# One conditioned transformer block on one core: half of the MLP's transposed rows are modulated by ScalarE instead of VectorE

## The chip, the core and the metric

The kernel runs on one core of one Trainium2 chip. The core has five engines that work beside each other: TensorE (PE, matrix products and transposes; PEld is its load of stationary operands), VectorE (DVE), ScalarE (ACT), GpSimd (POOL) and SyncE (SP), which issues most of the transfers. Each engine takes its own instructions in the order in which the program gives them, and semaphores hold an instruction back until those that it depends on, on other engines, have ended. Matrix products are written into PSUM, here in banks of 128 x 512 float32, and another engine carries them from there to SBUF.

The metric is the device time of the whole program in microseconds (us). It is the median of several executions; one more execution is taken with the hardware profiler.

## The reference: what is computed

The input x has 4 sequences of 1024 rows of 512 numbers, and each sequence has one conditioning vector of 512. First comes a graph attention layer over 20 neighbours per row. Its result goes through a transformer block that is modulated by the condition:

```python
mod = jax.nn.silu(c) @ W_mod + b_mod
sh_msa, sc_msa, g_msa, sh_mlp, sc_mlp, g_mlp = jnp.split(mod, 6, axis=-1)
x = x + g_msa * _attention(_modulate(_layernorm(x), sh_msa, sc_msa), W_qkv, W_out, b_out)
x = x + g_mlp * _ff(_modulate(_layernorm(x), sh_mlp, sc_mlp), W1, b1, W2, b2)
```

`_modulate(x, shift, scale)` is `x * (1 + scale) + shift`, with one shift and one scale for each of the 512 features of a sequence. `_ff` is `gelu(x @ W1 + b1) @ W2 + b2` with 2048 hidden features. The change concerns the modulation in the last of these lines. All is in float32.

## The kernel before

The kernel runs through three stages on the one core: the graph layer, the attention (with 16 heads, planned step by step by a list of fillers), and the MLP. The change lies in the MLP, which fills the last 780 us of the profile.

**Blocks.** The MLP goes over the 4096 rows in `NB2` = 8 blocks of 512 rows (`VB` = 4 tiles of 128 rows), in the loop over `k` at L1486. Each block has two parts on PE. The *up* part multiplies the block's rows with W1, in four groups `p`; the first two groups of block 0 were already done in the attention stage, so block 0 has only groups 2 and 3 here. The *down* part multiplies the hidden values with W2.

**Seven products.** Each group of the up part, and the whole down part, is a two by two block product that is done with seven products instead of eight (`seven`, L484). Its steps are a, c, b, a2, b2, d, b3, in that order on PE (`with_four`, L528). The up part uses the four PSUM banks `mau`, `mbu`, `mcu`, `mdu`, and the down part has four of its own, `mad`, `mbd`, `mcd`, `mdd`. In the up part a step has 8 products of 128 x 256, and in the down part it has 32. Step a ends with a copy of bank a to bank b by ScalarE (L519), and step c with a copy to SBUF, also by ScalarE (L508). The other banks are carried out by VectorE (L511, L515, L1539, L1544). The sums of operands that the seven products need are made by VectorE (`up_sums` L633, with L468 to L471) and by GpSimd (`mlp_rows` L600, with L476). In block 0 VectorE also makes the sums of W2 once (eight instructions at L476 that write `w2x` and `w`).

**The next block's rows.** While block k runs, the rows of block k+1 are loaded into `xl` (L379) and normalized in place by VectorE (`norm_rows`, L389). They then have to stand with features on the partitions, in the tile `hT`. That is done in `between()` (L1520), which is called right after step a of the down part has been emitted (L1552 to L1555). For each of the `FC` = 4 chunks of 128 features `norm_T` (L397) puts four transposes on PE (L407), which fill one PSUM bank, and one instruction that reads the bank, multiplies by the scale, adds the shift and writes the chunk of `hT`:

```python
if on_act:
    nc.scalar.activation(hT[st, k][:, c, :], pt, AF.Identity, scale=scale, bias=shift)   # L412
else:
    nc.vector.tensor_scalar(hT[st, k][:, c, :], pt, scale, shift, ALU.mult, ALU.add)     # L414
```

The banks are two of the up part's, which are free at that time. `new_bank` (L1475) gives them in turn: chunks 0 and 2 are transposed into `mcu`, chunks 1 and 3 into `mau`. So the transposes of chunk 2 wait until chunk 0 has been read, and those of chunk 3 until chunk 1 has been read. Since PE takes its instructions in order, step c of the down part (bank `mcd`) stands behind all sixteen transposes.

After the transposes `between()` gives SP the loads of the block's residual rows (`rows2`, L1530; these reuse the buffers of `xl`, so they wait for the transposes that read them), GpSimd the four sums of `mlp_rows` over the new `hT`, and then GpSimd four additions of a bias to the residual rows (L1534). The sums are needed by the up part of the next block, the residual rows by L1544 at the end of steps a2, b2, d and b3.

**Order.** The order of the instructions on each engine is that of the program's text: the schedule is written by hand. Block 7 has no next rows, so there are 7 places where `norm_T` is called in the MLP, for k = 0 to 6. `norm_T` is also used for the attention's rows and for the MLP's first rows; there it is called with its default, `on_act=True`.

Of the kernel before, what the change touches and what calls it, by code (L numbers as in the profile page):

```python
# [41 lines left out]
def cond_block_kernel(  # L42
# [71 lines left out]
    def rstd(rs, mv, nm, a, b):  # L114

        nc.scalar.activation(rs[:, a:b], mv[:, a:b, 1], AF.Sqrt, bias=eps)
        nc.vector.reciprocal(rs[:, a:b], rs[:, a:b])
        nc.vector.scalar_tensor_tensor(nm[:, a:b], mv[:, a:b, 0], -1.0, rs[:, a:b], ALU.mult, ALU.mult)

    def spread(k, b, o):  # L120

        nc.sync.dma_start(o, gated[32 * k + b : 32 * k + b + 1, :].broadcast_to([P, F]))
# [9 lines left out]
    with ExitStack() as gctx:  # L132
# [243 lines left out]
        def norm_load(st, k):  # L376
            for i in range(k * VB, (k + 1) * VB):
                t = rp.tile([P, F], F32, name="xl", tag="xl", bufs=VB)
                nc.sync.dma_start(t, NORM[st][0][i])  # L379
                xl[st, i] = t  # L380
# [12 lines left out]
        def norm_rows(st, k, on_act=False):  # L393
            for i in range(k * VB, (k + 1) * VB):
                norm_row(st, i, on_act)

        def norm_T(st, k, c, bank, on_act=True):  # L397

            sh, sc = NORM[st][4:]
            b = k * VB // NT  # L400
            if st == 1 and k > 0:
                hT[st, k] = hT[st, 0]
            elif c == 0:
                hT[st, k] = rp.tile([P, FC, VB * P], F32, name="hT", tag="hT", bufs=2)
            pt = bank("ptn")
            for n in range(VB):
                nc.tensor.transpose(  # L407
                    pt[:, n * P : (n + 1) * P], xl[st, k * VB + n][:, c * P : (c + 1) * P], ident
                )
            scale, shift = modT[:, sc + c, b : b + 1], modT[:, sh + c, b : b + 1]  # L410
# [4 lines that stand above are left out]
# [58 lines left out]
        def steps_b(e, o, b11, b12, b21, b22):  # L473

            return [
                lambda o=o_, i=i, j=j: e.tensor_tensor(o, i, j, ALU.subtract)  # L476
                for o_, i, j in ((o[0], b12, b11), (o[1], b22, o[0]), (b12, b22, b12), (o[2], b21, o[1]))
            ]
# [49 lines left out]
        def with_four(**kw):  # L528

            parts = seven(**kw)  # L530

            def step(n):
                for f in parts[n]:
                    f()

            return [lambda n=n: step(n) for n in ("a", "c", "b", "a2", "b2", "d", "b3")]
# [63 lines left out]
        def mlp_rows():  # L600

            h = hT[1, 0]
            if "mlp" not in tx:
                tx["mlp"] = xp.tile([P, 6, F], F32, name="tx", tag="tx")
            o = [tx["mlp"][:, k, :].rearrange("p (c r) -> p c r", c=2) for k in range(3)]
            sums_b(nc.gpsimd, o, h[:, :2, :HB], h[:, :2, HB:], h[:, 2:, :HB], h[:, 2:, HB:])
# [5 lines left out]
        def up_lhs(p):  # L612
            return lambda which, q, c: of_weights(2 * p + q, w1g[2 * p + q], which, c)
# [7 lines left out]
        def hidden(p, i, j):  # L621

            k = 2 * (2 * j + i)
            return hs[p][:, k : k + 2, :].rearrange("p q r -> p (q r)")

        def gelu(p, i, j, t):
            o = hidden(p, i, j)
            for q in (1, 0):
                m = i * MC // 2 + 2 * p + q
                cols = slice(q * HB, (q + 1) * HB)  # L630
                nc.scalar.activation(o[:, cols], t[:, cols], AF.Gelu, bias=vecs[:, V_1 + m : V_1 + m + 1])

        def up_sums(p):  # L633
            h = [hs[p][:, 2 * k : 2 * k + 2, :] for k in range(4)]
            sums_a(nc.vector, [hx[p][:, k] for k in range(3)], *h)
# [280 lines left out]
    with ExitStack() as actx:  # L916
# [14 lines left out]
        def bank(name):  # L931
            return ps.tile([P, F], F32, name=name, **MM)
# [40 lines left out]
        def short():  # L973
            return op_.tile([P, F], F32, name="s", tag="s", bufs=1)
# [457 lines left out]
    with ExitStack() as mctx:  # L1432
# [53 lines left out]
        for k in range(NB2):  # L1486
            b = k * VB // NT
            nxt = k + 1
            if nxt < NB2:
                norm_load(1, nxt)  # L1490
            for p in range(2 if k == 0 else 0, 4):
                steps = with_four(
                    get=up_banks.get, short=short, lhs=up_lhs(p), rhs=up_rhs, nk=2,
                    room=lambda: hidden(p, 1, 1), done=lambda i, j, t: gelu(p, i, j, t),
                )
                for n, f in enumerate(steps):
                    f()
                    if k == 0 and n == (4 if p == 2 else 2):

                        for j in ((0, 1) if p == 2 else (2,)):  # L1500
                            up_sums(j)
                if k > 0:
                    up_sums(p)
                elif p == 3:
                    sums = []
                    for j in range(2):
                        o = [w2x[j][:, n] for n in range(3)]
                        q, r = w2s[j], w2s[2 + j]
                        sums.append(steps_b(nc.vector, o, q[:, :, :HB], q[:, :, HB:], r[:, :, :HB], r[:, :, HB:]))
                    for n, two in enumerate(zip(*sums)):  # L1510
                        for f in two:
                            f()
                        if n == 0:
                            up_sums(p)
                if p == 1 and k == 1:
                    rstd(rs2, mv2, nm2, 3 * NT, NTA)
                if p == 2 and nxt < NB2:
                    norm_rows(1, nxt)

            def between():  # L1520
                if nxt < NB2:
                    for c in range(FC):
                        norm_T(1, nxt, c, new_bank, on_act=False)
                if k * VB % NT == 0:
                    spread(2, b, gate2)
                    spread(3, b, bias2)
                for n in range(VB):
                    i = k * VB + n
                    rows2[n] = rp.tile([P, F], F32, name="x2", tag="xl", bufs=VB)
                    nc.sync.dma_start(rows2[n], x2d[i])  # L1530
                if nxt < NB2:
                    mlp_rows()
                for n in range(VB):
                    nc.gpsimd.tensor_tensor(rows2[n], rows2[n], bias2, ALU.add)  # L1534

            def dn_done(i, j, t):
                y = t if (i, j) == (1, 1) else short()
                g = gate2[:, j * HB : (j + 1) * HB].unsqueeze(1).to_broadcast([P, 2, HB])
                nc.vector.tensor_tensor(  # L1539
                    y.rearrange("p (t f) -> p t f", t=2), t.rearrange("p (t f) -> p t f", t=2), g, ALU.mult  # L1540
                )
                for n in range(2):
                    o = rows2[2 * i + n][:, j * HB : (j + 1) * HB]
                    nc.vector.tensor_tensor(o, o, y[:, n * HB : (n + 1) * HB], ALU.add)  # L1544
                    if (i, j) in ((0, 1), (1, 0)):
                        at = k * VB + 2 * i + n
                        nc.sync.dma_start(out[at * P : (at + 1) * P, :], rows2[2 * i + n])

            steps = with_four(
                get=dn_banks.get, short=short, lhs=dn_lhs, rhs=dn_rhs, nk=MC // 2, room=None, done=dn_done  # L1550
            )
            for n, f in enumerate(steps):  # L1552
                f()
                if n == 0:
                    between()  # L1555
# [50 lines left out]
```

## Time and profile before

| | |
|---|---|
| median of 3 runs | 3081.66 us (3077.66 to 3081.82) |
| profiled execution | 3081.5 us, its span 3079.7 us |
| PE busy | 3039.7 us, 99% of the span |
| DVE busy | 1984.5 us, 64% |
| ACT busy | 1421.3 us, 46% |
| POOL busy | 1188.8 us, 39% |
| mean granted TensorE clock | 0.998 |
| L414, DVE, 128 x 512 out of PSUM | 28 instructions, 801 to 811 ns each |
| L412, ACT, the same work in the earlier stages | 36 instructions, 760 to 788 ns each |

The page gives the busy time of each engine, a strip of 40 slices, the chain of work that ended last, and the costliest groups of instructions. The span is the time from the first to the last instruction; the rest of the execution's time lies around it. In the timeline each row holds one instruction or several alike that follow on each other: start, length, engine, line, operation, what it writes and reads, how many, and in square brackets the idle time of that engine before it, with what ended that time. The length of a row of matmuls goes to the modelled end of the last one; the next row can start earlier, since they are pipelined. The granted clock is given as a fraction of the full speed.

### The profile page before, as it was taken

The numbers are of one execution on the slowest core, as the hardware profiler recorded it, in microseconds if no ns is written. First come the engines' busy times: TensorE is split into PE (matmuls) and PEld (weight loads), VectorE is DVE, ScalarE is ACT, GpSimd is POOL, SyncE is SP. The second block draws the span as 40 slices with busy tenths as digits, with TensorE's granted clock in tenths as the row PEclk, the third lists the DMA queues.
The fourth block names the chain that finished last, engine by engine and source line by source line (L and its number), as shares of the span: only waits on it lengthen the run. The fifth ranks groups of instructions, "written<-read, shape, count | busy, mean of one in ns | idle before, by whom it ended". The sixth has DMA issues, their size and how long they took to land.

```text
span 3079.7 us, 40763 instructions
## 1 busy us (share of the span) xinstructions
PE 3039.7 (99%) x14977; PEld 1918.1 (62%) x14977; DVE 1984.5 (64%) x2772; ACT 1421.3 (46%) x2351; POOL 1188.8 (39%) x729
## 2 busy tenths in 40 slices
PE   9999999999999999999999999999999999999999
PEld 5666655455455455455455455455468888888888
DVE  3788867777878777878777877777864332223222
ACT  2344446555655555755555755555641221112211
POOL 1444446445454555454654454654531100111010
PEclk9999999999999999999999999999999999999999
DMA  6343438676877776877776877776872011101110
GB/s 193 117 138 106 134 83 200 158 173 156 198 182 177 181 176 158 198 180 176 183 175 157 199 181 175 187 173 150 194 190 88 21 39 37 48 14 42 35 41 14
DMA packets 281882, 418.00 MB, mean 136 GB/s; under 512 B 28272, under 2 KB 100012, under 8 KB 281684
## 3 DMA queue, kind: packets, MB, share of 16 engines
q1 hardware_dynamic: 281436, 415.05, 53.1%
q8 instruction: 120, 1.97, 0.2%
q14 instruction: 78, 0.64, 0.1%
q10 hardware_dynamic: 248, 0.34, 0.0%
HBM read 121.09 MB, written 25.76 MB: 48 GB/s over the span
## 4 chain that ended last, share of the span: by engine, by line
PE 80%; DVE 7%; ACT 4%; issue 3%; POOL 2%; DMA 2%; SPq 2%; POOLq 0%; ACTq 0%; DVEq 0%
PE q L497 17%; PE psc L1079 14%; PE pav L1041 13%; PE pout L1059 6%; PE mbd L497 5%; PE mbu L497 5%; PE mad L497 3%; PE mau L497 3%; ACT w L1096 2%; PE mcd L497 2%; PE mdd L497 2%; PE mdu L497 2%; PE mcu L497 2%; POOL t L733 1%; DVE mx L1090 1%
## 5 line engine op out<-in xcount | busy, mean ns | idle before, releaser
L1105 POOL TENSOR_SCALAR w<-w,sm 128x1024 f32<-128x1024 f32 x256 | 733.9, 2867 | 874.7 <-DVE sm L1101 874.5
L1096 ACT ACTIVATE w<-psc,mx 128x1024 f32<-128x1024 f32 x512 | 570.6, 1114 | 643.0 <-DVE mx L1090 642.5
L1114 DVE STREAM_TRANSPOSE wd<-w 128x1024 f32<-128x1024 f32 x512 | 633.5, 1238 | 126.1 <-ACT w L1103 111.0
L1090 DVE TENSOR_REDUCE mx<-psc 128x1 f32<-128x1024 f32 x512 | 599.6, 1211 | 119.7 <-PE psc L1079 117.6
L1079 PE MATMUL psc<-kT,qT 64*128 64x512 f32 x2048 | 535.8, 617 | 7.8 <-ACT w L1096 5.0
L1041 PE MATMUL pav<-wT,v 128*64 128x256 f32 x4096 | 475.7, 382 | 1.5 <-DMA wT<-wd 1.4
L1041 PEld LDWEIGHTS pav<-wT,v 128*64 128x64 f32 x4096 | 289.0, 137 | 226.2 <-issue 64.8
L1079 PEld LDWEIGHTS psc<-kT,qT 64*128 64x128 f32 x2048 | 203.5, 186 | 264.3 <-issue 145.3
L1103 ACT ACTIVATE w<-w,sm 128x1024 f32<-128x1024 f32 x256 | 291.0, 1137 | 0.0
L1059 PE MATMUL pout<-wout,oT 128*128 128x512 f32 x512 | 245.6, 609 | 0.0
L476 POOL TENSOR_TENSOR tx<-hT 128x512 f32<-128x512 f32 x8 | 10.2, 1271 | 601.1 <-DVE hT L414 601.1
L497 PE MATMUL q<-hT,wqk 128*128 128x512 f32 (+1 forms) x396 | 182.6, 585 | 4.4 <-DVE q L511 4.4
L1059 PEld LDWEIGHTS pout<-wout,oT 128*128 128x128 f32 x512 | 90.2, 189 | 134.0 <-issue 119.2
L710 PE MATMUL pa<-kp,sfT 128*128 128x320 f32 x512 | 143.5, 433 | 1.4 <-ACT sfT L685 1.4
L519 ACT COPY mbu<-mau 128x512 f32<-128x512 f32 x30 | 17.1, 570 | 276.4 <-PE mau L497 276.4
L1067 DVE TENSOR_TENSOR xr<-pout,xr 128x512 f32<-128x512 f32 x128 | 85.5, 678 | 79.6 <-PE pout L1059 79.5
L497 PEld LDWEIGHTS q<-hT,wqk 128*128 128x128 f32 x396 | 73.5, 190 | 100.7 <-issue 87.3
L497 PE MATMUL q<-tx,ex 128*128 128x512 f32 (+1 forms) x264 | 125.0, 597 | 1.0 <-POOL tx L476 1.0
L710 PEld LDWEIGHTS pa<-kp,sfT 128*128 128x128 f32 x512 | 94.8, 190 | 38.2 <-ACT sfT L685 1.9
L670 PE MATMUL pf<-wx,xT 128*128 128x512 f32 x256 | 116.5, 598 | 0.9 <-DVE pf L659 0.9
L497 PE MATMUL mad<-w,hs 128*128 128x256 f32 x512 | 113.1, 379 | 0.0
L497 PEld LDWEIGHTS mad<-w,hs 128*128 128x128 f32 x512 | 97.3, 190 | 13.2
(285 smaller groups left out, 4221.9 us busy)
## 6 DMA issues: line engine op xcount, KB each, us to landing
wT<-wd SPq DMA_DIRECT2D x1024, 256.0 KB
wqk<-in_w_qkv SPq DMA_DIRECT2D x64, 256.0 KB
xT<-in_xt SPq DMA_DIRECT2D x32, 256.0 KB
xs<-in_x SPq DMA_DIRECT2D x32, 256.0 KB
x1d<-xs SPq DMA_DIRECT2D x32, 256.0 KB
xl<-x1d SPq DMA_DIRECT2D x32, 256.0 KB
wv<-in_w_qkv SPq DMA_DIRECT2D x32, 256.0 KB
xr<-x1d SPq DMA_DIRECT2D x32, 256.0 KB
```

The lines of the kernel that those rows point to most:

```text
L497: nc.tensor.matmul(t[:, q * width : (q + 1) * width], lhsT=lhs(which, q, k), rhs=rhs(which, q, k), start=(fresh and q == 0 and k == 0), st ...
L670: nc.tensor.matmul(pfs[i], lhsT=xT[i][:, c, :], rhs=wx[:, c, :], start=False, stop=(c == FC - 1), skip_group_check=True,)
L710: nc.tensor.matmul(pas[i][:, n, :HF], lhsT=sfT2[i][:, c, :], rhs=kp[:, b, c, n * HF : (n + 1) * HF], start=False, stop=(c == FC - 1), skip ...
L1041: nc.tensor.matmul(po[j * D : (j + 1) * D, :], lhsT=vt[b, g][:, m, p * P + j * D : p * P + (j + 1) * D], rhs=w[:, j, :, m, :], start=(m == 0),
L1059: nc.tensor.matmul(po, lhsT=oT[b, 2 * g + p][:, n * P : (n + 1) * P], rhs=wout[b, g][:, p, :], start=(p == 0), stop=(p == 1),)
L1067: nc.vector.tensor_tensor(t, po, t, ALU.add)
L1079: nc.tensor.matmul(sc[j][:, n * F : (n + 1) * F], lhsT=qT[b, gp][q, t * P : (t + 1) * P], rhs=kT[b, gp][q, n * F : (n + 1) * F], start=Tru ...
L1090: nc.vector.tensor_reduce(mx, sc, axis=AX.X, op=ALU.max, negate=True)
L1096: nc.scalar.activation(w, sc, AF.Exp, bias=mx, accum_out=sm)
L1103: nc.scalar.mul(w, w, sm)
L1105: nc.gpsimd.tensor_scalar(w, w, sm, None, ALU.mult)
L1114: nc.vector.transpose(wd[j][:, :, at, :], wn.pop((b, gp, t, j)).rearrange("p (m k) -> p m k", k=U))
```

## The change

One argument in `between()` changes. Before, all four chunks of the next rows are read out of PSUM by VectorE (L414). After it, block 0 has all four read by ScalarE (L412), and in blocks 1 to 6 chunks 1 and 3 are read by ScalarE and chunks 0 and 2 by VectorE. On ScalarE the new instructions stand between the copy of `mad` to `mbd` (L519) and the copy of `mcd` (L508). The banks, the transposes, PE's order, SP's order and GpSimd's order stay as they were. In number, 16 instructions go from VectorE to ScalarE.

```diff
@@ -1520,7 +1520,7 @@
             def between():
                 if nxt < NB2:
                     for c in range(FC):
-                        norm_T(1, nxt, c, new_bank, on_act=False)
+                        norm_T(1, nxt, c, new_bank, on_act=(k == 0 or c % 2 == 1))
                 if k * VB % NT == 0:
                     spread(2, b, gate2)
                     spread(3, b, bias2)
```

## The prediction

> **What bounds the kernel now.** I read the page first, then the chain of waits, PE's waits, and the timeline around the places that the change touches.
>
> ```profile
> span 3079.7 us, 40763 instructions
> ...
> PE 3039.7 (99%) x14977; PEld 1918.1 (62%) x14977; DVE 1984.5 (64%) x2772; ACT 1421.3 (46%) x2351; POOL 1188.8 (39%) x729
> ...
> PE 80%; DVE 7%; ACT 4%; issue 3%; POOL 2%; DMA 2%; SPq 2%; POOLq 0%; ACTq 0%; DVEq 0%
> ```
>
> PE is busy 99% of the span, and in the MLP the chain that ends last runs along PE from block to block. So the change is worth only what it takes from PE's waits. PE's own waits name the place:
>
> ```profile
> PE mcu L407 <- DVE hT L414: 5.0, 7, 2.2
> ```
>
> Seven times PE waits with a transpose into `mcu` until VectorE has read that bank: 5.0 us in all, 2.2 at the worst. The timeline shows why. First block 0:
>
> ```profile
> 2333.80 0.60 PE L407 MATMUL mcu<-ident,xl 128*128 128x128 f32 x4
> 2333.86 2.35 DVE L476 TENSOR_TENSOR w2x<-w,w2x 128x1024 f32<-128x1024 f32 x2
> 2333.99 0.57 ACT L519 COPY mbd<-mad 128x512 f32<-128x512 f32 x1 [6.07 <-PE mad L497]
> ...
> 2334.23 0.60 PE L407 MATMUL mau<-ident,xl 128*128 128x128 f32 x4
> 2336.13 0.81 DVE L414 TENSOR_SCALAR hT<-mcu,modT 128x512 f32<-128x512 f32 x1
> 2336.85 0.80 DVE L414 TENSOR_SCALAR hT<-mau,modT 128x512 f32<-128x512 f32 x1
> ...
> 2336.99 0.66 PE L407 MATMUL mcu<-ident,xl 128*128 128x128 f32 x4 [2.16 <-DVE hT L414]
> ...
> 2337.71 1.12 PE L407 MATMUL mau<-ident,xl 128*128 128x128 f32 x4
> ...
> 2338.62 8.25 PE L497 MATMUL mcd<-w2x,hx 128*128 128x256 f32 x32
> ...
> 2346.71 7.07 PE L497 MATMUL mbd<-w2x,hx 128*128 128x256 f32 x32
> ```
>
> Call the four groups of transposes T0 to T3 and their reads E0 to E3. T0 is done at 2334.40, but VectorE is busy with the sums of W2 until 2336.21, so T2 starts only at 2336.99. After that wait PE is slow: step c takes 8.09 us to the start of step b instead of 6.91. The granted clock, in windows of that time:
>
> ```profile
> 2337.50:2338.00 0.50, 0.44 (x4) 0.29 (x3) 0.46 (x2) 0.00 (x0) 0.26 (x1) 0.58 0.00 0
> ...
> 2340.00:2341.00 1.00, 1.00 (x4) 0.82 (x3) 0.00 (x0) 0.00 (x0) 1.00 (x1) 0.50 1.02 381
> ```
>
> The third number from the right is the clock: half speed from about 2337.6 to 2341. Windows of 4 us over the whole span show it below 0.995 at three places only, at 88, from 428 and here (0.70 and 0.88 in the two windows from 2336, which is 0.30 x 4 + 0.12 x 4 = 1.68 us lost), and these are the three places after the start where PE idled 2.0 us or more (2.20, 2.00, 2.16); after the next longest idles (1.35, 1.09) it stayed full. Then block 1, which blocks 2 to 6 repeat to within 0.02 us:
>
> ```profile
> 2436.49 0.60 PE L407 MATMUL mcu<-ident,xl 128*128 128x128 f32 x4
> 2436.69 0.57 ACT L519 COPY mbd<-mad 128x512 f32<-128x512 f32 x1 [6.07 <-PE mad L497]
> ...
> 2436.93 0.60 PE L407 MATMUL mau<-ident,xl 128*128 128x128 f32 x4
> 2437.13 0.81 DVE L414 TENSOR_SCALAR hT<-mcu,modT 128x512 f32<-128x512 f32 x1 [5.58 <-PE mcu L407]
> 2437.86 0.80 DVE L414 TENSOR_SCALAR hT<-mau,modT 128x512 f32<-128x512 f32 x1
> ...
> 2438.00 0.66 PE L407 MATMUL mcu<-ident,xl 128*128 128x128 f32 x4 [0.47 <-DVE hT L414]
> ...
> 2438.72 0.65 PE L407 MATMUL mau<-ident,xl 128*128 128x128 f32 x4
> ...
> 2439.21 7.07 PE L497 MATMUL mcd<-w2x,hx 128*128 128x256 f32 x32
> ```
>
> Here VectorE starts E0 0.04 us after T0's end, and E1 right behind E0. T2 starts 0.06 us after E0's end, T3 0.06 after E1's, and step c 0.49 after T3. Groups that follow on each other without a wait stand 0.44 apart (T0 to T1).
>
> **Blocks 1 to 6.** E0 stays on VectorE, so T2 stays at 2438.00. E1 goes to ScalarE, where the copy L519 ends at 2437.26, before T1 does (2436.93 + 0.60 = 2437.53). So E1 starts at about 2437.57. The same instruction in the earlier stages took 760 to 788 ns; with 0.77 E1 ends at 2438.34 and lets T3 go at 2438.40. T3 can't start before T2 has passed, 0.49 after its start: 2438.49. That is now what is late, not the read. Behind T2 without a wait, T3 takes 0.44, so step c starts at 2438.93, against 2439.21: 0.28 us saved in each block, 6 x 0.28 = 1.7 us. E2 and E3 lie beside step c. No row shows both engines reading two banks at once, so bounds: if E1 took 1.09 it would end when VectorE ended it (2438.66) and save 0; below T2's end nothing more is to be had, so 0.28 is the top. I take the top, since all 36 rows of this instruction lie under 0.79, and up to 0.86 would still give it.
>
> [...]
>
> **Block 0.** All four reads go to ScalarE, past the sums of W2. L519 runs from 2333.99 to 2334.56. A second ScalarE instruction starts about 0.10 before the first one's recorded end (266.43 + 0.57 copy, the next at 266.90), so E0 starts at 2334.46, just after T0's end at 2334.40. E0 ends at 2335.23, T2 starts at 2335.29. E1 follows 0.68 behind E0 (1.46 for a row of two), ends at 2335.91, and T3 starts at 2335.97. Step c starts 0.49 later, at 2336.46, against 2338.62: 2.16 saved. PE's wait before T2 becomes 2335.29 - 2334.83 = 0.46 us, like the other blocks' 0.47, after which the clock stayed full six times out of six. So step c takes 6.91 instead of 8.09: another 1.18. Together 3.34 us. The distance between blocks agrees: from T0 of block 0 to T0 of block 1 it is 102.69, between the later ones 99.41.
>
> The bounds are the handover from ScalarE to PE (0.05 to 0.15 us: at 428.26 a ScalarE read ends, its 0.19 us accumulator read at 428.36, and PE goes at 428.41), at most 0.2 us in this block, and the clock: if the slow stretch came all the same, its 1.68 us would be left and the block would save 1.66.
>
> **Waits added or moved.** Step c's first product in block 0 now has a wait on VectorE of its own. Its operands were written by 2329.4; even if it waited for the last sum of W2 (2336.21), that is before 2336.46. Next in line would be this one: it has 0.2 us of cover. L412 waits for PE, and in blocks 1 to 6 for GpSimd's old reads of `hT`, done 90 us before (GpSimd idles 90.37 there). Behind the reads on ScalarE stands only L508, which waits for PE until 2446.32 with 9.05 idle before it; on VectorE L511, idle 13.07. No transfer moves past another: SP's four loads L1530 wait for the transposes, so they go up to 2 us earlier; they and GpSimd's L1534, over by 2449.0, are first read at 2460.93 in block 1. GpSimd's sums start earlier and are needed at 2480. So all of that costs nothing.
>
> **Sum.** 3.34 + 1.68 = 5.0 us. The profiled execution took 3081.5 us (span 3079.7), 0.16 under the median, so the forecast is **3076.5 us**, 0.16% less than before. What a measurement of this kernel can tell from no change is about 0.2%, 6.2 us, so this is just inside.
>
> **Rivals.**
>
> *The clock drops in block 0 anyway.* Then 5.02 - 1.68 = 3.3 us: 3078.2. For it: three cases are few, and the length of the idle time need not be all. Against it: the three longest idle times and the three drops are the same places. [...]
>
> *More is saved than summed.* If PE had no wait at all between T0 and step c, it would take 4 x 0.44 = 1.76 instead of 2.72: 0.96 x 6 + (4.82 - 1.76 + 1.18) = 10.0, or 3071.5. Against it: E0 still has to end before T2. Reads in parallel that hand over earlier would give some of it, 7 us at most: 3074.5.
>
> *The runs fall on the lower level.* One of the three runs shown is 4.0 us under the others, about as much as the drops at 88 and 428 cost together. If the median falls there: 3081.5 - 4 - 5 = 3072.5.
>
> *Slower: ScalarE has to change its function table* between Gelu and this function. A table load is 1283 ns. In blocks 1 to 6 it would run from 2437.26, E1 would end at 2439.31, T3 start at 2439.37, step c at 2439.86: 0.65 lost in each, 3.9 in all, with block 0 still 0.78 better: 3084 to 3085. It gets beyond 0.2% from the point where PE's longer waits also halve the clock in each block (1.68 x 7 more): 3096. Against it: the changed program's ScalarE order holds no further load, and among the 36 earlier ones, that lie between Exp instructions, the profile has none at L412.
>
> **How the numbers follow.** The forecast gets 0.54, the clock drop 0.10, more saved 0.14, the lower level 0.16, the table 0.06. The first two lie within 0.2%, the third and fourth are faster, and the table is slower beyond 0.2% in most of its chance: faster 0.30, same 0.65, slower 0.05. The range runs from the lower level to a little above the clock's case: 3072.0 to 3079.5. The forecast's own range is 3075.7 to 3077.5.
>
> **What would show it.** In the profile after: in block 0 T2 about 1.5 us behind T0, step c 2.66 us behind T0 and 6.91 long, with the clock at 1.00; the distance to the next block's T0 at 99.35 instead of 102.69. In blocks 1 to 6 step c 2.44 us behind T0 instead of 2.72, T3 with no idle time before it, and the distance at 99.13. PE's waits before T2 go from 5.0 us to about 2.8 on L414 (six times) and 0.5 on L412 (once). It would be wrong if E1 on ScalarE took over 1.1 us, if a table load stood at L412 or before the next Gelu, or if the clock fell in another place.

## The result, and the profile after

The changed kernel took 3075.82 us (median of 21 runs, 3071.61 to 3078.84), the kernel before 3079.84 in the same comparison (21 runs, 3073.88 to 3082.91). The ratio is 0.9986, with a 95% interval of 0.9981 to 0.9992: between 2.5 and 5.9 us faster. That is within the 0.2% that the prediction called hard to tell from no change, and the interval of the ratio does not reach 1. The forecast was 3076.5 us and 5.0 us saved. The profiled execution after took 3076.57 us, 4.9 less than the profiled one before.

Two lines of the page after, its span and its busy times:

```profile
span 3074.8 us, 40782 instructions
...
PE 3037.0 (99%) x14977; PEld 1920.7 (62%) x14977; DVE 1971.7 (64%) x2756; ACT 1435.7 (47%) x2367; POOL 1187.5 (39%) x729
```

VectorE lost 16 instructions and 12.8 us of work, ScalarE gained 16 and 14.4 us. Neither number is the gain; PE's waits are. In the list of PE's waits after the change (time in all, times, longest), the group of seven waits with 5.0 us has become these two:

```profile
PE mcu L407 <- DVE hT L414: 2.8, 6, 0.5
...
PE mcu L407 <- ACT hT L412: 0.5, 1, 0.5
```

The timeline of block 0 after the change (start, length, engine, line, operation, what it writes and reads, count, and the idle time before it):

```profile
2333.72 0.60 PE L407 MATMUL mcu<-ident,xl 128*128 128x128 f32 x4
2333.85 2.35 DVE L476 TENSOR_TENSOR w2x<-w,w2x 128x1024 f32<-128x1024 f32 x2
2333.92 0.57 ACT L519 COPY mbd<-mad 128x512 f32<-128x512 f32 x1 [6.06 <-PE mad L497]
...
2334.41 0.79 ACT L412 ACTIVATE hT<-mcu,modT 128x512 f32<-128x512 f32 x1
2335.08 0.79 ACT L412 ACTIVATE hT<-mau,modT 128x512 f32<-128x512 f32 x1
...
2335.25 0.65 PE L407 MATMUL mcu<-ident,xl 128*128 128x128 f32 x4 [0.49 <-ACT hT L412]
...
2335.92 0.66 PE L407 MATMUL mau<-ident,xl 128*128 128x128 f32 x4
...
2336.41 7.07 PE L497 MATMUL mcd<-w2x,hx 128*128 128x256 f32 x32
...
2343.32 2.97 PE L497 MATMUL mbd<-w2x,hx 128*128 128x256 f32 x13
```

VectorE is still busy with the sums of W2, and the reads no longer stand behind them. T2 follows T0 by 1.53 us instead of 3.19, step c follows T0 by 2.69 instead of 4.82, and step c is 6.91 long (2336.41 to 2343.32) instead of 8.09. Block 1, like blocks 2 to 6:

```profile
2433.11 0.60 PE L407 MATMUL mcu<-ident,xl 128*128 128x128 f32 x4
...
2433.54 0.60 PE L407 MATMUL mau<-ident,xl 128*128 128x128 f32 x4
2433.75 0.81 DVE L414 TENSOR_SCALAR hT<-mcu,modT 128x512 f32<-128x512 f32 x1 [5.58 <-PE mcu L407]
2434.24 0.78 ACT L412 ACTIVATE hT<-mau,modT 128x512 f32<-128x512 f32 x1 [0.36 <-PE mau L407]
...
2434.61 0.66 PE L407 MATMUL mcu<-ident,xl 128*128 128x128 f32 x4 [0.47 <-DVE hT L414]
...
2435.11 0.63 PE L407 MATMUL mau<-ident,xl 128*128 128x128 f32 x4
...
2435.57 7.07 PE L497 MATMUL mcd<-w2x,hx 128*128 128x256 f32 x32
```

ScalarE's read of chunk 1 now overlaps VectorE's read of chunk 0. T3 has no wait of its own any more, and step c stands 2.46 us behind T0 instead of 2.72. From T0 to the next block's T0 it is 99.39 us in block 0 (before: 102.69) and 99.16 in the later ones (before: 99.41). That is 3.30 + 6 x 0.25 = 4.8 us, and the first T0 came 0.08 earlier: together all of the 4.9 us between the two spans. Both profiled executions had the clock at one half at 88 us (for 3.41 us) and behind the wait that ends at 428 (for 6.83 us), so these falls don't enter the difference; only the one before had it fall in block 0 (3.41 us).

So the time went where the forecast put it. Open was how much of it comes in every execution, since 1.68 us of it hang on the clock, and whether the engine that reads matters or only the wait for a bank. The runs below ask this. Their ratios are to the kernel before on the same chip.

### The profile page after: what moved, and what is told of

Same layout as the page of the kernel before. It is cut to its first block, busy times and chain, and to the rows that moved or that the text cites. A ratio compares the mean times of both kernels' runs of the same rounds, so it can differ in the third digit from the quotient of the medians.

```text
span 3074.8 us, 40782 instructions
## 1 busy us (share of the span) xinstructions
PE 3037.0 (99%) x14977; PEld 1920.7 (62%) x14977; DVE 1971.7 (64%) x2756; ACT 1435.7 (47%) x2367; POOL 1187.5 (39%) x729
## 4 chain that ended last, share of the span: by engine, by line
PE 81%; DVE 7%; ACT 4%; issue 3%; POOL 2%; DMA 2%; SPq 1%; POOLq 0%; ACTq 0%; DVEq 0%
PE q L497 17%; PE psc L1079 14%; PE pav L1041 13%; PE pout L1059 6%; PE mbd L497 5%; PE mbu L497 5%; PE mad L497 4%; PE mau L497 3%; ACT w L1096 2%; PE mcd L497 2%; PE mdd L497 2%; PE mcu L497 2%; PE mdu L497 2%; DVE mx L1090 1%; POOL t L733 1%
## 5 line engine op out<-in xcount | busy, mean ns | idle before, releaser
L519 ACT COPY mbu<-mau 128x512 f32<-128x512 f32 x30 | 17.2, 572 | 276.5 <-PE mau L497 269.8
```

## The experiments

**Each part alone.** Block 0 alone, `on_act` in `between()`:

```diff
-                        norm_T(1, nxt, c, new_bank, on_act=False)
+                        norm_T(1, nxt, c, new_bank, on_act=(k == 0))
```

> ScalarE reads all four chunks in block 0; in blocks 1 to 6 VectorE reads all four as before. Theory (two separate savings: in block 0 the reads leave the queue behind the sums of W2 and the clock stays up; in blocks 1 to 6 two engines read side by side): block 0 as in the profile after, 2.69 us from T0 to step c and 6.91 for step c, blocks 1 to 6 as before, 2.72; 3.3 us faster than before, ratio 0.9989. Rival (the clock's drop in block 0 is chance and not the idle time of PE): the drop is there in some runs, 1.6 to 3.3 us faster.

Measured: ratio 0.9990 (0.9981 to 0.9999). In the profile step c follows T0 by 2.68 us in block 0 and is 6.91 long; in blocks 1 to 6 it follows by 2.71 to 2.72 as before. And the other part alone:

```diff
-                        norm_T(1, nxt, c, new_bank, on_act=False)
+                        norm_T(1, nxt, c, new_bank, on_act=(k > 0 and c % 2 == 1))
```

> VectorE reads all in block 0 as before; in blocks 1 to 6 ScalarE reads chunks 1 and 3. Theory: 0.26 to 0.28 us saved in each of six blocks, 2.46 from T0 to step c; block 0 keeps its 2.2 us wait, its half clock and 8.1 us for step c; 1.6 to 1.7 us faster than before, ratio 0.9995. Rival (the saving comes from VectorE having less to do anywhere): more than 1.7 us.

Measured: ratio 0.9996 (0.9987 to 1.0005), which by itself can't be told from no change. The profile tells more: 2.46 to 2.47 us from T0 to step c in blocks 1 to 6, 99.15 to 99.16 from block to block, and in block 0 the old picture, 4.90 us with step c 7.95 long. The two parts don't touch each other, and each is close to what the prediction's sum gave it: from T0 to T0, block 0 alone saves 3.3 us (99.38 instead of 102.69) and each later block 0.25. In these profiles nothing is left that a relieved VectorE would have to explain.

**No ScalarE, another place in VectorE's queue.** In block 0 the last four sums of W2 are emitted behind the reads:

```diff
                     for n, two in enumerate(zip(*sums)):
+                        if n >= 2:
+                            w2_rest.extend(two)
+                            continue
                         for f in two:
                             f()
...
                         norm_T(1, nxt, c, new_bank, on_act=False)
+                while w2_rest:
+                    w2_rest.pop(0)()
```

> No work for ScalarE at all: VectorE keeps all the reads, but in block 0 the last four of its eight sums of W2 are emitted behind the four reads. Theory: what block 0 loses is the place in VectorE's queue, not the engine: T2 follows T0 by about 1.5 us, no half clock, step c 2.7 us behind T0 and 6.91 long, 3.3 us faster than before, as with ScalarE in block 0 alone. Rival (ScalarE is the quicker reader of PSUM): no faster than before in block 0's reads, so 1.7 us at the most.

Measured: ratio 0.9992 (0.9983 to 1.0001). Block 0 in the timeline:

```profile
2336.12 0.60 PE L407 MATMUL mcu<-ident,xl 128*128 128x128 f32 x4
...
2336.76 0.81 DVE L414 TENSOR_SCALAR hT<-mcu,modT 128x512 f32<-128x512 f32 x1 [2.69 <-PE mcu L407]
...
2337.63 0.66 PE L407 MATMUL mcu<-ident,xl 128*128 128x128 f32 x4 [0.47 <-DVE hT L414]
...
2338.84 7.07 PE L497 MATMUL mcd<-w2x,hx 128*128 128x256 f32 x32
...
2339.78 3.42 DVE L476 TENSOR_TENSOR w<-w,w 128x1024 f32<-128x1024 f32 x2
```

T2 is 1.51 us behind T0, step c 2.72 and 6.91 long, and the next T0 follows after 99.42. That is nearly all of what ScalarE gave in block 0 (99.38), without ScalarE. So block 0's loss was the place of the reads in VectorE's queue. The time by itself can't separate 3.3 us from none: the interval holds both, and the two medians (3079.19 and 3079.37) are almost the same. Here the timeline decides.

**All on ScalarE.**

```diff
-                        norm_T(1, nxt, c, new_bank, on_act=False)
+                        norm_T(1, nxt, c, new_bank, on_act=True)
```

> ScalarE reads all four chunks in all seven blocks. Theory (in blocks 1 to 6 the saving is that two engines read side by side): one engine again reads chunk 1 behind chunk 0; T3 waits for the end of that read, step c 2.65 to 2.70 us behind T0 in blocks 1 to 6 against 2.72 before and 2.46 after the change; block 0 as after the change; 3.3 to 3.7 us under before. Rival (ScalarE is the quicker reader): 2.46 or less in every block.

Block 1 of that kernel:

```profile
2428.98 0.60 PE L407 MATMUL mcu<-ident,xl 128*128 128x128 f32 x4
...
2429.68 0.78 ACT L412 ACTIVATE hT<-mcu,modT 128x512 f32<-128x512 f32 x1
2430.36 0.77 ACT L412 ACTIVATE hT<-mau,modT 128x512 f32<-128x512 f32 x1
2430.51 0.66 PE L407 MATMUL mcu<-ident,xl 128*128 128x128 f32 x4 [0.49 <-ACT hT L412]
2431.18 0.66 PE L407 MATMUL mau<-ident,xl 128*128 128x128 f32 x4
2431.67 2.54 PE L497 MATMUL mcd<-w2x,hx 128*128 128x256 f32 x11
```

Step c stands 2.69 us behind T0, and 2.69 to 2.70 in all of blocks 1 to 6. One engine that reads both banks gives 2.69 if it is ScalarE and 2.72 if it is VectorE; the two side by side give 2.46. So in blocks 1 to 6 the saving is the overlap of two reads, as expected, and the choice of the one engine is worth only 0.03. The single execution took 3073.92 us against 3082.06 of the kernel before beside it. That is more than the 3.3 to 3.7 us expected, and it has another cause, which lies ahead of the MLP's blocks: T0 of block 0 comes at 2329.60, 4.2 us earlier than in the profile before. In this execution the clock fell nowhere until the program's last 2 us (granted 1.00 in every window of 4 us from 84 to 92 and from 424 to 436), though PE waited 2.21 us before 87.68 and 2.00 before 426.13, as it does in every profile of this study. That spoke against the prediction's reading of the clock, and the next runs are on that.

**How long must PE wait for the clock to fall?** The changed kernel, with idle copies put ahead of VectorE's reads:

```diff
+                    for _ in range(max(k - 1, 0)):
+                        nc.vector.tensor_copy(gates, dn_banks["ma"])
                     for c in range(FC):
```

> The changed kernel with idle reads added: in blocks 2, 3, 4, 5, 6 VectorE first copies the bank mad 1, 2, 3, 4, 5 times into a tile that nothing reads later, so that PE's wait before T2 grows from 0.47 us to about 0.6, 1.2, 1.9, 2.5 and 3.1. Theory (a wait of 2 us or more lets the clock fall to one half for 3.4 us, costing 1.7): clock full and step c 6.91 long in blocks 1 to 3, half clock and step c about 8.1 or more in blocks 5 and 6, block 4 open; about 10 to 13 us above the changed kernel. Rival (the drop is chance or depends on the phase alone): no relation to the length of the wait, and 8 us above it from the waits alone.

Measured: 3087.62 us. PE's waits came out longer than expected. By block, from the timeline:

| block | PE's wait before T2, us | step c behind T0, us | step c, us | granted clock |
|---|---|---|---|---|
| 0 | 0.48 | 2.68 | 6.91 | full |
| 1 | 0.47 | 2.46 | 6.91 | full |
| 2 | 1.23 | 3.19 | 6.91 | full |
| 3 | 1.95 | 4.49 | 8.02 | fell |
| 4 | 2.68 | 5.48 | 7.58 | fell |
| 5 | 3.40 | 5.37 | 6.90 | full |
| 6 | 4.13 | 6.93 | 8.50 | fell |

Block 5 is the surprise: 3.40 us of wait and a full clock. So neither theory holds as stated. No wait of the table up to 1.23 us brought the fall; of its four from 1.95 us up, three did. In blocks 3 and 4 the clock was at one half for 3.41 us, in block 6 for 6.83. Then the same wait six times over, twice:

```diff
+                if 0 < k and nxt < NB2:
+                    for z in (F, F, P):
+                        nc.vector.tensor_copy(gates[:, :z], dn_banks["ma"][:, :z])
                 if nxt < NB2:
                     for c in range(FC):
```

> The changed kernel with two and a quarter idle copies of mad on VectorE ahead of the reads in blocks 1 to 6, so that PE waits about 2.2 us before T2 in each of them, as in block 0 before the change. If the length of the wait alone decides on the clock: six half clocks, 1.7 us each, and about 20 us above the changed kernel. If the phase of some clock of its own decides as well, as the two full clocks after 2.0 and 2.2 us of wait and the one after 3.4 in the last runs suggest: some of the six, not all. Blocks without a half clock have step c 6.91 long.

> The same kernel once more. If the phase decides, the blocks with a half clock may be others than in the first run; if the place in the program decides, the same ones.

The two runs took 3092.28 and 3091.09 us. The wait was 2.28 us in each block (2.29 once). Of the clocks in blocks 1 to 6, five fell in the first run (blocks 2 to 6) and four in the second (3 to 6). The granted clock (third number from the right) in windows behind T2 of blocks 1 and 2 of the first run:

```profile
2433.00:2437.00 4.00, 3.89 (x22) 3.56 (x23) 0.86 (x2) 0.78 (x1) 3.07 (x3) 1.00 0.50 141
...
2534.00:2538.00 4.00, 3.95 (x15) 3.39 (x16) 0.81 (x1) 0.78 (x1) 2.90 (x3) 0.60 0.50 158
```

The distance to the next T0 is 100.95 us without the fall and 102.62 with it: a fall costs 1.67 us here, which at half speed is a slow stretch of 3.3 to 3.4 us. Block 2 differs between the two runs at the same wait and the same place in the program, so neither the length of the wait nor the place in the program decides alone. From one block to the next with a fall, the slow stretch begins 0.22 us earlier behind T0: in the first run step c starts 4.42, 4.64, 4.86 and 5.06 us behind T0 in blocks 2 to 5 while its own length shrinks from 8.41 by the same steps. 102.62 - 0.22 is 102.40, which is 30 times 3.413, and 3.413 us is also the length of the slow stretch in block 0 of the profile before, by that trace's record of the clock.

**Does block 0 lose its clock in every execution of the kernel before?** The kernel before, profiled twice more, with no edit.

> The kernel before, unchanged, for a second profile. The wait of 2.16 us before T2 in block 0 comes in every execution. If the phase decides on the clock, a profile of it can show step c 6.91 us long, and the change then saves 1.66 us less against it: 3.3 instead of 5.0.

> The same once more. Wait of 2.16 us in block 0 as before; the half clock there, and at 88 and 428 us, may come or not.

The two executions took 3079.98 and 3079.24 us. In the first, step c of block 0 took 8.11 us. In the second, T2 and step c:

```profile
2336.32 0.66 PE L407 MATMUL mcu<-ident,xl 128*128 128x128 f32 x4 [2.22 <-DVE hT L414]
...
2337.53 7.07 PE L497 MATMUL mcd<-w2x,hx 128*128 128x256 f32 x32
...
2344.44 1.89 PE L497 MATMUL mbd<-w2x,hx 128*128 128x256 f32 x8
```

The wait is 2.22 us, step c takes 6.91 (2337.53 to 2344.44), and the next T0 follows after 101.16 instead of 102.69. So there are executions of the kernel before in which block 0 keeps its clock; in the four profiles with this wait it fell three times. Against such an execution the change saves 1.77 + 6 x 0.25 = 3.3 us, not 4.9.

The traces also hold the times at which the granted clock changed. Within each trace they lie whole multiples of 3.4133 us apart, to within 0.02 us (in the profile before, the stretches at half speed begin at 88.20, 429.54 and 2337.59 us, which is 100 and 559 such lengths), so each trace can be cut into windows of that length. Where they lie against the program differs from execution to execution: one of them ends 0.60 us behind the start of T2 of block 0 in the profile before, and 1.45 us ahead of it in the second profile above. In these traces the fall went with how much of PE's idle time lay in one window. In the 14 traces, 40 windows at full clock held 2.0 us or more of PE's idle time, and all 40 ended with a fall (14 of them at the program's end). Before the 15 falls in the MLP's blocks the window held 1.95 to 2.38 us; the most that a window there held without a fall is 1.96. The 2.16 us of wait in the profile before lay in one window. The 2.22 us of the second profile above were cut by a window's end into 0.77 and 1.45, and the 3.40 us of block 5 into 1.94 and 1.46. This doesn't cover every fall: near 428 us four came with 1.28 to 1.89 us of idle time in the window. Nor do the traces show what in the chip brings the fall.

**A way without any wait.** If only the wait for a bank matters, more banks should do as well as a quicker read. The transposes go into four banks of the up part:

```diff
-            return up_banks[("ma", "mc")[len(flip) % 2]]
+            return up_banks[("ma", "mb", "mc", "md")[len(flip) % 4]]
```

> VectorE keeps all the reads in the old order; the four groups of transposes go into four banks (mbu, mcu, mdu, mau) instead of two in turn. Theory (only the wait for a bank matters, not who reads it): PE waits for no read, step c follows T0 by 4 x 0.44 = 1.76 us in every block, 0.96 saved in six blocks and 4.24 with the clock in block 0, together 10.0 us, ratio 0.9967; if step c's first product in block 0 waits for the last sum of W2, 0.8 us less. Rival (the time of the reads themselves counts): no more than the change saved, 5 us.

In this kernel every transpose opens its bank anew, that is, as the start of a new sum there. The up part later adds onto what stands in `mbu` and `mdu`, and the output is then off by a relative error of 0.026; with one opening of each bank, the second form below, it is not. That the additions fail in the columns of the earlier transposes is inferred from this, not shown. PE's instructions and their order in time are the same. Measured: ratio 0.9970 (0.9959 to 0.9981), 1.74 to 1.75 us from T0 to step c in all blocks. The second form opens each bank once:

```diff
-                nc.tensor.transpose(
-                    pt[:, n * P : (n + 1) * P], xl[st, k * VB + n][:, c * P : (c + 1) * P], ident
+                nc.tensor.matmul(
+                    pt[:, n * P : (n + 1) * P], lhsT=xl[st, k * VB + n][:, c * P : (c + 1) * P], rhs=ident,
+                    is_transpose=True, start=(n == 0), stop=True, skip_group_check=True,
                 )
```

> The four banks again, VectorE reads all; of the four transposes into a bank only the first opens it. Theory: the same instructions on PE, 1.75 us from T0 to step c in every block, 8.5 to 10.0 us faster than before, ratio 0.9967 to 0.9973; the same as the split transposes within 0.1%. Rival (the manner of opening costs time): T0 to step c above 1.8 us.

Measured: 3068.51 us against 3080.15, ratio 0.9964 (0.9952 to 0.9977). Block 1:

```profile
2429.33 0.60 PE L407 MATMUL mbu<-ident,xl 128*128 128x128 f32 x4
2429.77 0.60 PE L407 MATMUL mcu<-ident,xl 128*128 128x128 f32 x4
2430.20 0.60 PE L407 MATMUL mdu<-ident,xl 128*128 128x128 f32 x4
2430.64 0.60 PE L407 MATMUL mau<-ident,xl 128*128 128x128 f32 x4
2431.08 7.07 PE L498 MATMUL mcd<-w2x,hx 128*128 128x256 f32 x32
```

VectorE reads all four chunks in this kernel, as before the change, and PE doesn't see it. The last variant keeps two banks and moves chunks 2 and 3 behind step c:

```diff
-            def between():
+            def chunks(cs):
                 if nxt < NB2:
-                    for c in range(FC):
+                    for c in cs:
                         norm_T(1, nxt, c, new_bank, on_act=False)
+
+            def between():
+                chunks((2, 3))
...
                 f()
                 if n == 0:
+                    chunks((0, 1))
+                if n == 1:
                     between()
```

> VectorE keeps all the reads, two banks in turn as before; the transposes of chunks 0 and 1 stay behind step a, those of chunks 2 and 3, and all that between() does after them, go behind step c. Theory (PE pays only for waiting for a bank): the reads of chunks 0 and 1 lie beside step c, PE waits for none of them, step c follows T0 by 0.88 us and step b follows step c by 6.91 + 0.88; each block takes 98.44 us as with four banks, the half clock in block 0 is gone, 8.5 to 10.0 us faster than before, ratio 0.9967 to 0.9973. Rival (the later start of GpSimd's sums, 7 us, or of the loads of the residual rows reaches the path): a wait of PE or VectorE in step d or b3, or at the next up part, and less than that.

Measured: 3070.11 us against 3080.15, ratio 0.9970 (0.9958 to 0.9982). Block 1:

```profile
2430.48 0.60 PE L407 MATMUL mcu<-ident,xl 128*128 128x128 f32 x4
...
2430.91 0.60 PE L407 MATMUL mau<-ident,xl 128*128 128x128 f32 x4
...
2431.35 7.07 PE L497 MATMUL mcd<-w2x,hx 128*128 128x256 f32 x32
...
2438.26 0.60 PE L407 MATMUL mcu<-ident,xl 128*128 128x128 f32 x4
...
2438.70 0.60 PE L407 MATMUL mau<-ident,xl 128*128 128x128 f32 x4
...
2439.13 7.07 PE L497 MATMUL mbd<-w2x,hx 128*128 128x256 f32 x32
```

The reads of chunks 0 and 1 lie beside step c, so chunks 2 and 3 find their banks free. From block to block it is 98.44 us, the same as with four banks and 0.72 below the changed kernel. Nothing that starts later by it, GpSimd's sums or the residual rows, reaches PE. Both variants are faster than the kernel before. Against the changed kernel (0.9981 to 0.9992) the four banks are clear by the intervals, the split just touches its lower end; they were not timed on one chip with it, so this comparison runs over the kernel before. The two variants can't be told apart.

## Why the prediction was right, point by point

- **PE's waits alone make the difference.** Right. The two spans differ by 4.9 us, and the distances from T0 to T0 account for it.
- **Block 0.** The sum put T2 1.49 us behind T0, step c 2.66 behind T0 and 6.91 long. Measured: 1.53, 2.69 and 6.91. The first read started 0.69 us behind T0 instead of 0.66, and the reads took 0.79 instead of 0.77; a handover shorter by 0.01 and a read that followed 0.01 sooner leave 0.03. Step c's own wait on VectorE cost nothing: it starts 0.49 behind T3, as forecast, and the sums of W2 were done 0.2 us earlier.
- **Blocks 1 to 6.** Forecast 0.28 each from T3 following T2 without a wait, measured 0.26. T3 starts 0.49 to 0.50 us behind T2, which is the limit that the prediction named. Step c follows T2 by 0.96 us instead of the 0.93 in the sum. In block 2 of the run with growing waits, where chunk 1 had been read 0.85 us before T3, it is 0.93, so the read of chunk 1 still costs PE at most 0.03.
- **The clock.** Here the reading was too strong. The prediction took it that a wait of 2 us or more brings the fall and a short one doesn't, from three cases, and gave the rival that the length is not all a chance of 0.10. The short waits held: no clock fell after 1.37 us or less. The long ones did not: in the second further profile of the kernel before, in the run with all reads on ScalarE and in blocks of the runs with added waits the clock stayed full after 2.0 to 3.4 us. What the sum left out is where the wait lies in the windows of 3.413 us that the change times give (2.16 us of it in one window in the profile before, 1.45 at most in the second further profile). The 1.68 us in the sum are therefore a saving in some executions only. As an estimate from the figures above: if every position of the windows is equally likely, a wait of 2.2 us puts 1.95 us or more into one window in about half of the cases ((3.41 + 2.2 - 2 x 1.95) / 3.41), so the term was worth some 0.8 us on average and the sum 4.2. The wait in block 0 is now 0.49 us, and no wait of that length was followed by a fall. That the median saved 4.0 instead of 5.0 fits with this, but the interval (2.5 to 5.9) is too wide to show it.
- **The time itself.** That 3075.82 us lies only 0.7 from the forecast is partly luck: the forecast started from 3081.5, while the kernel before has a median of 3079.84 in this comparison, 1.7 lower, and the saving was 1.0 smaller than summed.
- **The rivals.** No further table load and no slower read appeared: the profile after has the same 12 table loads of 1283 ns as the one before, none at L412, and L412 took 775 to 788 ns in the MLP. "More saved than summed" did not happen in this kernel; its bound of 10.0 us was reached by other edits (11.6 and 10.0 us on the medians, of which PE's waits in the timeline explain up to 10). A level some 4 us lower is there in the runs: the 6 of 21 runs of the changed kernel with a mean granted clock of 1.000 average 3072.7 us, the 13 with 0.998 average 3076.9. It did not reach the median.

## What to carry to other kernels

When one engine is busy 99% of the time, look for the few places where it waits, and ask of each what stands ahead of the releasing instruction in its own engine's queue. A read out of PSUM that sits behind unrelated work can be moved to another engine, put earlier in the same queue, or be given time by moving the instruction that needs the bank; the last added no instruction here and gave about twice as much. A fall of the clock after a long wait (1.5 to 1.7 us here) is worth a term in the sum, but with a chance beside it: in this kernel a wait of 2.16 us brought the fall in one execution, and one of 2.22 us at the same place did not in another.

## What the runs showed of the hardware that was not expected

The clock's fall was not settled by the length of PE's wait: it came after waits of 1.95, 2.16, 2.28, 2.68 and 4.13 us, stayed away after 2.00, 2.22, 2.28 and 3.40 in other cases, and never came after 1.37 or less once the first products had run. In the MLP it went with the idle time inside one of the windows of 3.413 us: 1.95 to 2.38 us before the 15 falls, 1.96 at the most without one. A fall of one window cost 1.5 to 1.7 us there; the one of two windows, after the wait of 4.13 us, cost 2.4 (step c 0.83 us later and 1.59 longer than without a fall).

In the kernel with the sums of W2 behind the reads, these sums ran beside GpSimd's sums, and both became slower: VectorE's took up to 2.29 us each instead of 1.22, GpSimd's up to 2.25 instead of 1.27. Neither reached PE. GpSimd's sum that began at 2338.38, ahead of VectorE's, took 1.27 us, and the one that began at 2340.00, beside them, 2.11. What the two engines compete for, no run shows.
